# Three edits in a one-core decoder layer: list scatters without mutual waits, expert loads in pieces, an earlier start of cross attention

## The chip, the cores and the metric

The kernel runs on one core of a Trainium2 chip, as one program. A core has TensorE (PE in the profile; PEld is its weight load, which overlaps the matmuls), VectorE (DVE), ScalarE (ACT), GpSimd (POOL) and SyncE (SP, which here only issues DMAs). Each engine works through its own list of instructions in a fixed order. Engines meet through semaphores.

The metric is device time in microseconds (us), from launch to end. The inputs are float32, and the output must agree with the reference.

## The reference

One decoder layer on x of shape (4, 512, 512), which is 2048 tokens of width 512, in three residual parts:

```
x = x + deltanet(layernorm(x))            # gated delta rule, 16 heads of 128, causal convolutions
x = x + cross_attention(layernorm(x), ctx)    # 16 heads of 32, 256 context rows, fake-quantised q, k, v, weights
x = x + ffn(layernorm(x))
# ffn(t): 
h  = rmsnorm(t, ln1);  q, k, v = h @ wq, h @ wk, h @ wv     # 16 heads on 4 key/value heads of 128
x1 = t + causal_softmax(rope(rmsnorm(q)), rope(rmsnorm(k))) @ v @ wo
h2 = rmsnorm(x1, ln2)
sig = sigmoid(h2 @ router_w);  top 2 of 8 experts by sig + bias;  weights sig / sum
x1 + sum over the 2 experts of weight * (silu(h2 @ wg[e]) * (h2 @ wu[e])) @ wd[e]
```

Each token goes to two of eight experts. Which tokens an expert gets depends on the data.

## The kernel before

The tokens are 16 tiles of 128 (NT = 16), four to a sequence. The program has three stages in time.

**The first part** (0 to about 2190 us) is the delta rule, in pairs of heads, sequence by sequence. Cross attention of tiles 0 and 1 runs beside its end.

**The middle part** (about 2190 to 3650 us) is where all three edits act. Per tile i it has these generators, each of which issues a little work and yields:

- `cross(i)`: layernorm, the projection with wq, quantisation of q (`quantised`, whose last step is L217 on POOL), transposition through PE and ACT (`transposed`, L200 and L202), four rounds of scores, softmax over 256 context rows, quantisation of the weights (L274 on POOL, L278 on DVE), transposition (L287), product with the values (L300), projection (L318). `crossing(i)` also does `norms(i - 1)`, the two norms in front of the self attention of tile i - 1.
- `qkv(i)`: six projections of the tile (L1067) with weights that are loaded anew for each tile in halves of 512 KB into the four c_q buffers (L1034).
- `attention(i)`: scores (L1133), softmax, transposition (L1159), values (L1163), and the output projection (L1173) with weights loaded anew for each tile in eight pieces of 512 KB into three c_o buffers (L1043). Its last sum is L1199.
- `rest_of(i)`: the second norm, and the router's logits (L1230).
- `route(i0, n)`: the choice of experts for n tiles at a time, after tiles 3, 7, 11 (four tiles each), 14 (three) and 15 (one). DVE ranks the logits, PE counts places with small matmuls (L1257 to L1261), and then every token's two rows (its number and weight, 8 bytes) are scattered to their places in `lists` in HBM: one indirect DMA from POOL per tile and choice (L1282), so 8, 8, 8, 6 and 2 of them, 32 in all. `place` and `entry`, which hold rows and places, have two buffers each.
- `load_experts()`: waits until the last `crossing` and the last `qkv` have been issued, closes the pools `top` and `mid` that they used, and in the freed memory loads all weights of the eight experts: 24 DMAs of 512 KB on SP (L1305 to L1307).

**The last part** (from about 3640 us) gathers the lists (L1362 on POOL: one row of 128 entries for each of 39 blocks), gathers each block's tokens (L1388), applies the block's expert, and adds the result to `acc` in HBM. It ends with one copy to the output.

The order of the middle part is written out by `weave`. Every stream is a list of (start, length, generator, kind), in a virtual time whose unit is one tile of attention. A generator's steps are taken to be evenly spread over its length, with the step count of the last generator of its kind (`steps` has the first guess). `weave` always issues the step with the earliest virtual time. So attention(i) starts at i, qkv(i) at i - Q with Q = 1.36, crossing(i) at i - X with X = 2.75, rest_of(i) at i + 1.06, and load_experts at NT - Q = 14.64.

The order of issue is a priority, not yet the order on the engines. The framework lays out each engine's instructions ahead of time: among those whose inputs and buffers it takes to be ready, the one issued earliest comes first. So an instruction can stand much earlier on its engine than where it was issued. It also derives every wait from the tiles that are read and written. `lists` is one tensor for it, and so each scatter waits for the one before.

Of the kernel before, what the change touches and what calls it, by code (L numbers as in the profile page):

```python
# [40 lines left out]
NT = B * S // P  # L41
# [57 lines left out]
def decoder(ctx: ExitStack, tc: tile.TileContext, a: dict, out: bass.AP):  # L99
    nc = tc.nc  # L100
# [9 lines left out]
    def over(ap, n):  # L110

        return ap.unsqueeze(1).to_broadcast([P, n, ap.shape[1]])

    def along(ap, n):

        return ap.unsqueeze(2).to_broadcast([P, ap.shape[1], n])
# [22 lines left out]
    def chain(*gs):  # L139
        for g in gs:  # L140
            yield from g

    steps = {"cross": 38, "qkv": 12, "rest_of": 4, "route": 10, "load": 1}
    steps.update((f"attention{c}", n) for c, n in enumerate((37, 41, 53, 57)))

    def weave(*streams):


        todo = []
        for n, stream in enumerate(streams):  # L150
            stream = list(stream)
            todo.append([stream[0][0], n, 0, stream])
        while todo:
            t = min(todo, key=lambda t: t[:2])
            _, length, g, kind = t[3][0]
            try:
                next(g)
                t[0] += length / steps[kind]
                t[2] += 1
            except StopIteration:  # L160
                steps[kind] = max(t[2], 1)
                t[2] = 0
                del t[3][0]
                if t[3]:
                    t[0] = max(t[0], t[3][0][0])
                else:
                    todo.remove(t)
# [10 lines left out]
    def turns(*gs):  # L178

        gs = [(g, n) for g, n in gs if g is not None]  # L180
        while gs:
            left = []
            for g, n in gs:
                if all(next(g, gs) is not gs for _ in range(n)):
                    left.append((g, n))
            gs = left
            yield
# [774 lines left out]
    with ExitStack() as st:  # L962
# [37 lines left out]
        def norms(i):  # L1000


            x2 = x2s.pop(i)
            x3 = wq_.tile([P, D], F32, name="x3", bufs=1)
            yield from layernorm(x3.unsqueeze(1), x2.unsqueeze(1), small)
            nc.sync.dma_start(x3d[i], x3)
            h = wq_.tile([P, D], F32, name="h3", bufs=1)
            ss = small.tile([P, 1], F32, name="rms_s")
            nc.scalar.activation(h, x3, AF.Square, accum_out=ss)
            yield  # L1010
            r = small.tile([P, 1], F32, name="rms_r")
            rsqrt(r, ss, small, add=1e-6, mul=1.0 / D)
            yield
            nc.vector.scalar_tensor_tensor(h, x3, r, ln1, ALU.mult, ALU.mult)
            yield
            hTs[i] = transposed(h, wq_, "hT", bufs=2)
            yield
# [181 lines left out]
            nc.vector.tensor_tensor(x3, pw, x3, ALU.add)  # L1199
            xs[i] = x3  # L1200

        xs = {}
        lgt = keep.tile([P, NT, NE], F32, name="lgt")
        count = keep.tile([P, NE], F32, name="count")
        nc.vector.memset(count, 0.0)
# [28 lines left out]
        def route(i0, n):  # L1234

            shape = [P, n, NE]
            flat = lambda t: t.rearrange("p n e -> p (n e)")
            sig, key, w = (small.tile(shape, F32, name=k, bufs=1) for k in ("r_sig", "r_key", "r_w"))
            hot = [small.tile(shape, F32, name=f"r_hot{k}", bufs=1) for k in range(2)]
            m = small.tile([P, n], F32, name="r_m", bufs=1)  # L1240
            nc.scalar.activation(sig, lgt[:, i0 : i0 + n, :], AF.Sigmoid)
            nc.vector.tensor_tensor(key, sig, over(rb, n), ALU.add)

            for k in range(2):
                nc.vector.tensor_reduce(m, key, AX.X, ALU.max)
                nc.vector.tensor_tensor(hot[k], key, along(m, NE), ALU.is_equal)
                nc.vector.tensor_tensor(hot[k], hot[k], over(rank_row, n), ALU.mult)
                nc.vector.tensor_reduce(m, hot[k], AX.X, ALU.max)
                nc.vector.tensor_tensor(hot[k], hot[k], along(m, NE), ALU.is_equal)
                if k == 0:  # L1250
                    nc.vector.scalar_tensor_tensor(key, hot[0], MASKED, key, ALU.mult, ALU.add)
            nc.vector.tensor_tensor(key, hot[0], hot[1], ALU.add)
            yield

            pl = p_b.tile([P, n + 1, NE], F32, name="pb")
            for t in range(n):
                nc.tensor.matmul(pl[:, t, :], tab[:, C_BEFORE, :], key[:, t, :], start=True, stop=t == 0)  # L1257
                for u in range(t):
                    nc.tensor.matmul(pl[:, t, :], tab[:, C_ONES, :], key[:, u, :], start=False, stop=u == t - 1)
            for t in range(n):  # L1260
                nc.tensor.matmul(pl[:, n, :], tab[:, C_ONES, :], key[:, t, :], start=t == 0, stop=t == n - 1)  # L1261
            nc.vector.tensor_tensor(w, key, sig, ALU.mult)
            nc.vector.tensor_reduce(m, w, AX.X, ALU.add)
            nc.vector.reciprocal(m, m)
            nc.vector.tensor_tensor(w, w, along(m, NE), ALU.mult)
            base = small.tile([P, NE], F32, name="r_base", bufs=1)
            nc.vector.tensor_tensor(base, count, first_row, ALU.add)
            yield
            nc.vector.tensor_tensor(sig, pl[:, 0:n, :], over(base, n), ALU.add)
            nc.vector.tensor_tensor(count, count, pl[:, n, :], ALU.add)  # L1270
            place = small.tile([P, n, 2], mybir.dt.int32, name="r_place", bufs=2)
            entry = small.tile([P, n, 2, 2], F32, name="r_entry", bufs=2)
            for k in range(2):
                nc.vector.tensor_tensor(key, hot[k], sig, ALU.mult)
                nc.vector.tensor_reduce(m, key, AX.X, ALU.add)
                nc.vector.tensor_copy(place[:, :, k], m)
                nc.vector.tensor_copy(entry[:, :, k, 0], token[:, i0 : i0 + n])
                nc.vector.tensor_tensor(key, hot[k], w, ALU.mult)
                nc.vector.tensor_reduce(entry[:, :, k, 1], key, AX.X, ALU.add)
            for t in range(n):  # L1280
                for k in range(2):
                    nc.gpsimd.indirect_dma_start(  # L1282
                        lists[:, :],
                        bass.IndirectOffsetOnAxis(place[:, t, k : k + 1].bitcast(mybir.dt.uint32), 0),
                        entry[:, t, k, :],
                        None,
                        bounds_check=LISTS - 1,
                    )
                yield

        def crossing(i):

            g = cross(i)
            return chain(turns((norms(i - 1), 1), (itertools.islice(g, 6), 1)), g)

        def load_experts():

            while done[0] < 2:
                yield
            top.close()  # L1300
            mid.close()
            we = st.enter_context(tc.tile_pool(name="d_w", bufs=1, reuse_waits="tile"))
            gu, d = we.tile([P, NE, KD, 2, NI], F32, name="w_gu"), we.tile([P, NE, NI // P, D], F32, name="w_d")
            for e in range(NE):
                nc.sync.dma_start(gu[:, e, :, 0, :], a["d_wg"][e].rearrange("(k p) c -> p k c", p=P))  # L1305
                nc.sync.dma_start(gu[:, e, :, 1, :], a["d_wu"][e].rearrange("(k p) c -> p k c", p=P))
                nc.sync.dma_start(d[:, e, :, :], a["d_wd"][e].rearrange("(k p) c -> p k c", p=P))  # L1307
            experts_w.extend((gu, d))

        done, experts_w = [0], []  # L1310

# [3 lines left out]

        Q, X = 1.36, 2.75
        at_x = [(i - X, 1.0, crossing(i), "cross") for i in range(2, NT)]
        at_x[-1] = (*at_x[-1][:2], last(chain(at_x[-1][2], norms(NT - 1))), "cross")  # L1320
        at_q = [(i - Q, 1.0, qkv(i), "qkv") for i in range(NT)]
        at_q[-1] = (*at_q[-1][:2], last(at_q[-1][2]), "qkv")
        at_a = [(i, 1.0, attention(i), f"attention{i % TB}") for i in range(NT)]
        at_r = []
        for i in range(NT - 1):
# [4 lines left out]
                g, kind = chain(g, route(12, 3)), "route"  # L1330
            at_r.append((i + 1.06, 0.5, g, kind))
        run(norms(0))
        weave(at_a, at_q, at_x, at_r, [(NT - 1 - Q + 1, 0.1, load_experts(), "load")])
        w_gu, w_d = experts_w
        run(rest_of(NT - 1), route(NT - 1, 1))

# [22 lines left out]
        at = small.tile([P, 1], mybir.dt.int32, name="at", bufs=1)  # L1359
        nc.vector.tensor_copy(at, mine)  # L1360
        both_ = wa.tile([P, 4, P], F32, name="qT", bufs=6).rearrange("p a b -> p (a b)")[:, 0 : 2 * P]
        nc.gpsimd.indirect_dma_start(  # L1362
            both_[0:NBLK],
            None,
            lists.rearrange("(n s) c -> n (s c)", s=P),
            bass.IndirectOffsetOnAxis(at[0:NBLK, 0:1].bitcast(mybir.dt.uint32), 0),
            bounds_check=LISTS // P - 1,
        )
        nc.vector.tensor_scalar(be, be, float(NE - 1), None, ALU.min)
        who = small.tile([P, NBLK], mybir.dt.int32, name="who", bufs=1)  # L1370
        nc.vector.tensor_copy(who, be)
# [76 lines left out]
        for b in range(NBLK):  # L1448
            d = down(b)
# [65 lines left out]
```

## Time and profile before

| | |
|---|---|
| median of 3 runs | 3922.55 us (3909.57 to 3927.0) |
| the profiled execution | 3921.34 us, of which its span is 3919.6 us |
| mean granted clock of TensorE | 0.941 of full speed |
| POOL waited before L1282 for the landing of an earlier scatter | 62.8 us in 23 waits, the longest 5.1 us |
| landing of a scatter, from its issue | 2.2 to 7.8 us, median 5.2 us |
| landing of c_o loads, median | 4.1 us |
| landing of the expert loads, median by kind | 9.3, 10.0 and 9.6 us |

"Span" is from the first to the last instruction of the profiled execution. The profile page gives busy time by engine, the span in 40 slices, DMA queues, the chain that ended last, and groups of instructions with the idle time ahead of each and what ended it. In the notation `pb<-xnT,w` the tile left of the arrow is written, those right of it are read. A line `PE pb L200 <- POOL xn L217: 22.6, 5, 8.2` of the waits says that PE stood 22.6 us in total, 5 times, at most 8.2 us, ahead of instructions of line 200 that write `pb`, until POOL's line 217 had written `xn`. In a time line the columns are start, length, engine, line, operation, tiles, shapes and count, and in brackets the idle time ahead of it with what ended it.

The slices of the page, in fortieths of the span (98 us each), with PE's granted clock in tenths:

```profile
PE   5898899898989989898989799998998999897897
...
PEclk8899999899999998999999899998999999898898
```

The middle part begins at slice 23 of the 40.

### The profile page before, as it was taken

The page shows a single profiled execution, that of the slowest core. Times are in us where ns is not written, and L with a number is a line of the kernel's source. Part 1 is how long each engine was busy: PE and PEld are TensorE (multiplying, and loading weights), DVE is VectorE, ACT ScalarE, POOL GpSimd, SP SyncE. Part 2 cuts the span into 40 slices and gives each one's busy share as a digit, 9 for nine tenths or more (in the row PEclk, how much of TensorE's full clock was granted, in tenths as well). Part 3 has the DMA queues.
Part 4 walks back from the last instruction along what each step waited for, and adds up shares of the span by engine and source line. Part 5 has one row for each costly group of instructions (what it writes and reads, how often), then busy time and mean ns, then how long its engine had stood idle before and what let it go on. Part 6 is the DMA issues. An engine that isn't in the chain of part 4 may idle for free. (4 is left out here: it accounts for less than half of the span.)

```text
span 3919.6 us, 48951 instructions
## 1 busy us (share of the span) xinstructions
PE 3487.2 (89%) x16466; PEld 1984.1 (51%) x16466; DVE 2238.4 (57%) x5115; ACT 1522.5 (39%) x4190; POOL 1373.3 (35%) x1941
## 2 busy tenths in 40 slices
PE   5898899898989989898989799998998999897897
PEld 3455555555555555555555445554554555453343
DVE  5576657675766666756765466555665655543111
ACT  3434443334343434334333244443443444433121
POOL 1443554344435552455335222112212211210442
PEclk8899999899999998999999899998999999898898
DMA  5324332433243333343332444445444444445344
GB/s 163 107 77 123 98 103 80 130 101 111 82 119 119 98 100 106 97 119 104 96 98 87 158 145 154 137 132 132 146 127 137 153 146 139 141 152 183 79 82 93
DMA packets 391881, 465.56 MB, mean 119 GB/s; under 512 B 128451, under 2 KB 242115, under 8 KB 391440
## 3 DMA queue, kind: packets, MB, share of 16 engines
q1 hardware_dynamic: 380080, 438.03, 37.1%
q0 software_dynamic: 10112, 21.58, 3.1%
q8 instruction: 132, 2.16, 0.2%
q10 hardware_dynamic: 1440, 2.84, 0.2%
q14 instruction: 117, 0.96, 0.1%
HBM read 401.76 MB, written 64.81 MB: 119 GB/s over the span
## 5 line engine op out<-in xcount | busy, mean ns | idle before, releaser
L503 PE MATMUL pb<-xnT,w 128*128 128x512 f32 x2048 | 954.9, 605 | 0.0
L503 PEld LDWEIGHTS pb<-xnT,w 128*128 128x128 f32 x2048 | 381.9, 195 | 423.7 <-issue 419.7
L514 DVE SCALAR_TENSOR_TENSOR cv<-pb,pp,cv 128x511 f32<-128x511 f32 (+2 forms) x576 | 427.3, 742 | 153.0 <-ACT cv L511 144.2
L1067 PE MATMUL pb<-c_q,hT 128*128 128x512 f32 x768 | 362.9, 609 | 7.9 <-DMA c_q<-in_c_wq_dram 3.6
L644 POOL TENSOR_TENSOR iW<-iA,iT 32x31 f32<-32x31 f32 (+15 forms) x496 | 249.3, 503 | 210.3 <-DMA iA<-at_d 140.5
L825 PE MATMUL pb<-wot,og 128*128 128x512 f32 x512 | 264.9, 642 | 32.8 <-DVE og L796 26.5
L645 POOL TENSOR_TENSOR iT<-iT,iW 32x31 f32<-32x31 f32 (+15 forms) x496 | 275.1, 555 | 39.0
L1173 PE MATMUL pw<-c_o,oT 128*128 128x512 f32 x512 | 244.8, 611 | 21.9 <-DMA c_o<-in_c_wo_dram 15.5
L511 ACT ACTIVATE cv<-pb,pp 128x512 f32<-128x512 f32 x192 | 148.2, 772 | 261.2 <-PE pb L503 260.7
L1067 PEld LDWEIGHTS pb<-c_q,hT 128*128 128x128 f32 x768 | 143.8, 196 | 162.2 <-issue 149.4
L1139 ACT ACTIVATE e<-pb,nm,rq 128x128 f32<-128x128 f32 (+3 forms) x256 | 158.0, 626 | 104.2 <-DVE nm L1137 75.2
L274 POOL TENSOR_SCALAR x_e<-x_e 128x1024 f32<-128x1024 f32 x64 | 68.7, 1073 | 334.0 <-ACT x_e L269 256.6
L644 DVE TENSOR_TENSOR iW<-iA,iT 32x31 f32<-32x31 f32 (+15 forms) x496 | 178.4, 360 | 11.7 <-DMA iA<-at_d 0.2
L645 DVE TENSOR_TENSOR iT<-iT,iW 32x31 f32<-32x31 f32 (+15 forms) x496 | 177.4, 358 | 11.9
L269 ACT ACTIVATE x_e<-pb,nm 128x256 f32<-128x256 f32 x256 | 118.1, 475 | 164.2 <-DVE nm L266 160.7
L1163 PE MATMUL po<-eT,val 128*128 128x512 f32 x320 | 171.6, 630 | 10.0 <-ACT eT L1161 7.7
L1133 PE MATMUL pb<-kT,qT 128*128 128x256 f32 (+3 forms) x576 | 163.5, 410 | 3.6 <-ACT x_e L269 3.6
L558 POOL TENSOR_TENSOR rk<-ss,mhalf 128x8 f32<-128x8 f32 x32 | 53.1, 1659 | 322.0 <-DVE ss L557 321.9
L579 DVE SCALAR_TENSOR_TENSOR at<-pb,em 128x512 f32<-128x512 f32 x64 | 44.3, 692 | 199.9 <-ACT em L397 199.9
L1173 PEld LDWEIGHTS pw<-c_o,oT 128*128 128x128 f32 x512 | 94.4, 194 | 125.5 <-issue 92.1
L1420 PE MATMUL pb<-w_gu,eT 128*128 x312 | 142.7, 601 | 3.8 <-issue 3.8
L825 PEld LDWEIGHTS pb<-wot,og 128*128 128x128 f32 x512 | 89.7, 194 | 110.3 <-issue 53.3
(324 smaller groups left out, 6609.7 us busy)
## 6 DMA issues: line engine op xcount, KB each, us to landing
c_o<-in_c_wo_dram SPq DMA_DIRECT2D x128, 512.0 KB, 4.1
c_q<-in_c_wq_dram SPq DMA_DIRECT2D x128, 512.0 KB, 4.6
w<-in_a_w_dram SPq DMA_DIRECT2D x124, 512.0 KB, 3.7
row<-g_d SPq DMA_DIRECT2D x64, 512.0 KB, 3.8
at_d<-at SPq DMA_DIRECT2D x64, 256.0 KB, 4.2
T<-t_d SPq DMA_DIRECT2D x32, 512.0 KB, 6.1
X<-x_d SPq DMA_DIRECT2D x32, 512.0 KB, 6.1
rrow<-r_d SPq DMA_DIRECT2D x32, 512.0 KB, 4.7
```

The costliest lines, as they stand in the source:

```text
L503: nc.tensor.matmul(pj, wt[:, kd, p * P : (p + 1) * P], xnT[:, kd, :], start=kd == 0, stop=kd == KD - 1)
L511: nc.scalar.activation(ac, pj, AF.Identity, bias=cb[:, m, h : h + 1], scale=cw[:, m, h, 3:4])
L514: nc.vector.scalar_tensor_tensor(ac[:, j:], pj[:, : S - j], cw[:, m, h, 3 - j : 4 - j], ac[:, j:], ALU.mult, ALU.add)
L644: eng.tensor_tensor(u, A[:, i, i + 1 :].unsqueeze(2).to_broadcast([nb, n, w]), T[:, i, :w].unsqueeze(1).to_broadcast([nb, n, w]), ALU.mult)
L645: eng.tensor_tensor(T[:, i + 1 :, :w], T[:, i + 1 :, :w], u, ALU.add)
L825: nc.tensor.matmul(pw, og[p][:, c * P : (c + 1) * P], wot[:, p, :], start=p == 0, stop=p == HG - 1)
L1067: nc.tensor.matmul(pj, hT[:, kd, :], w[:, kd % 2, :], start=kd == 0, stop=kd == KD - 1)
L1133: nc.tensor.matmul(ps[:, m, k * P : (k + w) * P], qT[g][:, n + m, :], kT[:, g, j : j + w, :], start=True, stop=True)
L1139: nc.scalar.activation(e[n + m][:, :nk], ps[:, m, :nk], AF.Exp, bias=nm[:, n + m : n + m + 1], scale=rq, accum_out=es[:, n + m : n + m + 1])
L1163: nc.tensor.matmul(po, val[:, g, :], eT, start=k == 0, stop=k == c)
L1173: nc.tensor.matmul(pw, oT[:, h + m, :], w[:, m, :], start=g == 0 and h + m == 0, stop=g == 3 and h + m == 3)
L1420: nc.tensor.matmul(pg, hT[:, kd, :], w_gu[:, bass.ds(e, 1), kd, :, :], start=kd == 0, stop=kd == KD - 1)
```

## The change

There are three edits, and the diff is whole but for context.

1. The scatters of `route` are put into one group whose members need not wait for each other, with the reason that each row is written once. Their names are kept in `entered`. The gather of the lists gets an explicit dependence on each of the 32.
2. `load_experts` yields after every DMA, its tiles are handed out before the loads, and its stream gets the length 0.9 and 26 assumed steps where it had 0.1 and 1. Its start is the same number: NT - 1 - Q + 1 is NT - Q.
3. `crossing(i)` starts at 2 - 3.1 + (i - 2) 1.03 and has the length 1.03. It started at i - 2.75 with the length 1.

```diff
-    steps = {"cross": 38, "qkv": 12, "rest_of": 4, "route": 10, "load": 1}
+    steps = {"cross": 38, "qkv": 12, "rest_of": 4, "route": 10, "load": 26}
...
-        xs = {}
+        xs, entered = {}, []
...
-                    nc.gpsimd.indirect_dma_start(
+                    ins = nc.gpsimd.indirect_dma_start(
                         lists[:, :],
                         bass.IndirectOffsetOnAxis(place[:, t, k : k + 1].bitcast(mybir.dt.uint32), 0),
                         entry[:, t, k, :],
                         None,
                         bounds_check=LISTS - 1,
-                    )
+                    ).ins
+                    tc.declare_no_dep(ins, group="entries", reason="a row is written once")
+                    tc.add_to_no_dep_group("entries", ins)
+                    entered.append(ins.name)
                 yield
...
+            experts_w.extend((gu, d))
+
             for e in range(NE):
                 nc.sync.dma_start(gu[:, e, :, 0, :], a["d_wg"][e].rearrange("(k p) c -> p k c", p=P))
+                yield
                 nc.sync.dma_start(gu[:, e, :, 1, :], a["d_wu"][e].rearrange("(k p) c -> p k c", p=P))
+                yield
                 nc.sync.dma_start(d[:, e, :, :], a["d_wd"][e].rearrange("(k p) c -> p k c", p=P))
-            experts_w.extend((gu, d))
+                yield
...
-        Q, X = 1.36, 2.75
-        at_x = [(i - X, 1.0, crossing(i), "cross") for i in range(2, NT)]
+        Q, X, W = 1.36, 3.1, 1.03
+        at_x = [(2 - X + (i - 2) * W, W, crossing(i), "cross") for i in range(2, NT)]
...
-        weave(at_a, at_q, at_x, at_r, [(NT - 1 - Q + 1, 0.1, load_experts(), "load")])
+        weave(at_a, at_q, at_x, at_r, [(NT - Q, 0.9, load_experts(), "load")])
...
-        nc.gpsimd.indirect_dma_start(
+        ins = nc.gpsimd.indirect_dma_start(
             both_[0:NBLK],
             None,
             lists.rearrange("(n s) c -> n (s c)", s=P),
             bass.IndirectOffsetOnAxis(at[0:NBLK, 0:1].bitcast(mybir.dt.uint32), 0),
             bounds_check=LISTS // P - 1,
-        )
+        ).ins
+
+        for name in entered:
+            tc.add_manual_dep(ins, name, mybir.DependencyInfo(mybir.DependencyClass.Sync, mybir.DependencyReason.DATA), reason="entries")
```

## The prediction

> **What bounds the kernel now.** I read the busy rows first, then TensorE's waits in the last stage (2190 to 3650 us, where attention, projections, cross attention and routing are woven), then the time lines around each long wait.
>
> ```profile
> PE 3487.2 (89%) x16466; PEld 1984.1 (51%) x16466; DVE 2238.4 (57%) x5115; ACT 1522.5 (39%) x4190; POOL 1373.3 (35%) x1941
> ...
> PE pb L200 <- POOL xn L217: 22.6, 5, 8.2
> PE pw L1173 <- DMA c_o<-in_c_wo_dram: 15.5, 1, 15.5
> ...
> PE pb L287 <- DVE rsq L122: 9.1, 1, 9.1
> ```
>
> TensorE (PE) is busy 89%, and 93 to 100% in most 20 us windows of this stage, so the stage's time is PE's work plus its idle time. Two causes make most of that: c_o, and what comes over POOL. The POOL time line at the third full routing shows why:
>
> ```profile
> 3375.58 1.03 POOL L1282 DMA_INDIRECT lists<-r_entry,r_place  x1 [2.86 <-DMA lists<-r_entry,r_place]
> 3379.79 0.99 POOL L1282 DMA_INDIRECT lists<-r_entry,r_place  x1 [3.18 <-DMA lists<-r_entry,r_place]
> 3380.81 1.05 POOL L217 TENSOR_TENSOR xn<-xn,fq_s 128x512 f32<-128x512 f32 x1
> ```
>
> Each scatter waits for the landing of the one before, with POOL stopped; L217 stands behind five of them. PE then waits 8.2 us, and comes back at a lower clock:
>
> ```profile
> 3381.92 1.11 PE L200 MATMUL pb<-tab,xn 128*128 128x128 f32 x4 [8.25 <-POOL xn L217]
> ...
> 3360.00:3380.00 20.00, 13.67 (x42) 6.64 (x40) 8.82 (x30) 4.23 (x13) 6.51 (x8) 0.84 0.50 108
> 3380.00:3400.00 20.00, 18.08 (x56) 9.75 (x57) 8.19 (x18) 6.10 (x20) 7.29 (x9) 0.68 0.20 53
> 3400.00:3420.00 20.00, 19.89 (x78) 9.69 (x80) 9.95 (x23) 9.42 (x30) 4.98 (x6) 1.00 0.71 218
> ```
>
> (Window, length, busy PE, PEld, DVE, ACT, POOL, granted PE clock, DMA share, GB/s.) In the second row PE is busy 18.1 us, but at clock 0.68: four transposes take 1.11 us where 0.60 is usual.
>
> The other cause, on SP's queue and on PE:
>
> ```profile
> 3552.93 1.65 SPq L1307 DMA_DIRECT2D w_d<-in_d_wd_dram  x1
> 3554.68 13.11 SPq L1043 DMA_DIRECT2D c_o<-in_c_wo_dram  x4
> ...
> 3546.41 1.98 PE L1163 MATMUL po<-eT,val 128*128 128x512 f32 x4 [0.29 <-ACT eT L1161]
> 3563.90 3.49 PE L1173 MATMUL pw<-c_o,oT 128*128 128x512 f32 x4 [15.51 <-DMA c_o<-in_c_wo_dram]
> ```
>
> The 24 expert loads leave from 3523.71 to 3554.68; the c_o load that PE needs goes behind them and lands 9.2 us after (median 4.1).
>
> **The change, step by step** (against the profiled run, 3921.3 us).
>
> *Scatters.* Per routing I add PE's idle time, from its waits, and the excess of cold matmuls over the same rows at full clock.
> - First (2656 to 2724): waits 9.1+2.5+2.3+0.7+0.3 = 14.9; cold: L287 1.08 for 0.60, L1173 3.45 for 1.88 and 6.71 for 3.60, together 5.2. Sum 20.1.
> - Second (3012 to 3052): waits 8.1+1.8; cold L200, L1163, L262 2.0. Sum 11.9.
> - Third (3356 to 3404): wait 8.2; cold L200, L1159, L262, L1163, L1075 and eight L1067 (5.51 for 3.60), 5.8. Sum 14.0.
>
> Cold matmuls at 2655.87 and 3358.87 follow the routing's own small matmuls and stay.
>
> Afterwards a scatter costs POOL its issue only. The nearest row is that of the independent row gathers (L1388), 1.32 us apart (1.01 busy, 0.30 between). On generation the Trainium skill ("DMA: Bandwidth & Descriptors", Anatomy of one DMA) says many descriptors can be emitted before their cost shows; that would leave nothing of the stalls and give all 46.0. The row decides: eight scatters hold POOL 8 x 1.32 = 10.6 us, and POOL executes in order, so a part stays. In the second and third routing the block (3360.5 + 10.6 = 3371.1) ends before L217's input is due (about 3373): I leave 2 and 3. In the first, L274's input is ready near 2677 and the second half of the entries only at 2663.6 (VectorE), and DVE's copy into r_entry (L1277) still waits for the buffer's readers to land (9.07 us at 2703.06 now): I leave 5. Gain 15+10+11 = **36**; bounds -7 (three times a block of 10.6 for a stall of 8.2) and 46.
>
> On the cold part the skill ("TensorE: Matmul & The Clock Gate", Part 1) has a half clock after an idle window of about 3.4 us, for about one busy window. By that a gap over 3.4 us costs 1.7 us; three gaps 5.1, where the rows show 5.2+2.0+5.8 = 13.0. With the rule the routings would lose 38.1 instead of 46.0 in all and the gain be near 29. I take the rows: in the third, matmuls are still slow at 3389, seven us after the gap.
>
> *Expert loads in 24 steps.* The loads get virtual time 14.64 to about 15.5 instead of one instant. They wait for nothing but the freed pools, as before; a c_o load issued between them is ahead of later pieces. c_o's buffer was free at 3541.4 (L1173 from 3539.57, 1.88); 4.1 to 9.2 us later is 3545.5 to 3550.6, against PE's need at 3548.4. So of 15.5 + cold 1.6 (3.49 for 1.88) = 17.1 I leave 2: gain **15**, bounds 0 (c_o cannot go later than behind all 24, where it is now) and 17.1. Late next is route(12, 3), at 3579.84 (PE waits 2.27 for DVE), which moves with it. Traffic now is 313 and 360 GB/s in the two 20 us windows from 3520; the same 12.6 MB over some 60 us is 210, plus c_o. The pieces stand behind c_o loads that wait for PE (29.06 us for four from 3577.60), and the first expert matmul is at 3647.60: even the last piece, due at half of attention(15), about 3577, has 70 us.
>
> *End.* Two scatters and the gather are a chain: 3629.58, 3633.41, 3636.84. The second's entry is ready at 3631.0, so it goes 2.2 us sooner, and all that follows with it. The gather now waits for all 32 scatters by name. Behind it on POOL stand the 39 row gathers, and PE for those. Of the 32, 30 landed by about 3610; a satisfied wait costs about 0.05 us (median semaphore row of L1277), 1.6 us at most, inside the 2.44 us that the gather waits anyway. Gain **2**, bounds 0.6 and 2.2.
>
> *Cross attention.* Starts move from i - 2.75 to 1.03 i - 3.16: 0.35 tile sooner at i = 2, 0.04 later at i = 15. The last cross with its norms ends near 13.45, before qkv(15) at 13.64. Before attention 0 PE has gaps, and the longest is cross(2)'s own:
>
> ```profile
> 2260.37 1.12 PE L200 MATMUL pb<-tab,xn 128*128 128x128 f32 x4 [5.26 <-POOL xn L217]
> ```
>
> With 0.9+0.7+0.4 beside it, 7.2 us idle, and cold L200, L262, L1067 0.5+1.0+1.2 = 2.7: 9.9. Under qkv(0)'s matmuls (3.60 us a group) that chain is covered; but its loads (xi, 256 KB) and stores (x3d, x2d) enter SP's queue before c_q loads for which PE already waited 3.6 us at 2232. I take half, **5**, bounds -4 and 9.9.
>
> Sum 36+15+2+5 = **58**: 3921.3 - 58 = 3863; the median of the runs is 1.2 above the profiled run, so **3864**.
>
> **Rivals.**
> - *The loads still leave as a lump* (all 24 are ready at the same moment, and SP is idle between c_o loads, which speaks for it; that a c_o load goes ahead of later pieces speaks against). The 15 are lost: 3879.
> - *The scatters become a block that holds POOL*: 10.6 us is more than the 8.2 us stalls. For it: POOL's order is fixed beforehand, and eight scatters are ready together. Against: in two of three routings the block ends in time. 36 lost: 3900.
> - *Slower: cross attention falls badly against attention.* Each tile has one chain L217 to L200 like the prelude's, where PE stood 5.3 us; in steady tiles it is now under 1. If the new phase opens it in 14 tiles, 14 x 5.3 = 74, against a gain of 53 elsewhere: 3943. It decides from 53 / 14 = 3.8 us a tile on. Against it: the shift is at most 0.35 tile, and the chain keeps its length and its neighbours.
> - *All stalls go*: 46+17.1+2.2+9.9 = 75: 3847.
>
> **Chances.** Forecast 0.57, lump 0.17, block 0.14, all gone 0.06, slower 0.06. 0.5% (20 us) is about what a measurement can tell from no change; the block case lies at that edge, half of it within. Range 3843 to 3895: from all gone to near the block. Faster 0.87, same 0.07, slower 0.06.
>
> **What would show it.** L1282 about 1.3 us apart, no L1282 waiting for a landing; PE's waits on L217 near 22.6 - 16 - 5 = 2 us; clock rows of 1.00 where 0.68 to 0.84 stood; c_o loads between expert loads, and PE's 15.5 us wait under 3; the gather 5 us after the first scatter of the last routing instead of 7.3. Wrong if SP issues the 24 loads unbroken, if L217 or L274 stands behind six scatters or more, or if PE's waits in tiles without routing grow past 3.8 us.

## The result and the profile after

The changed kernel took **3872.77 us** (median of 6 runs, 3865.23 to 3880.07), the kernel before beside it 3922.27 us (6 runs): a ratio of 0.9877, 95% interval 0.9855 to 0.9899. The forecast was 3864.0, with a range of 3843 to 3895. In a later comparison the same changed kernel made 3864.12 against 3920.55 (0.9855, 0.984 to 0.987). So the change is worth some 50 to 56 us.

The profiled execution took 3875.28 us, its span 3873.5 us. Its busy row and its slices of TensorE (PE), with the granted clock:

```profile
PE 3479.9 (90%) x16466; PEld 1984.5 (51%) x16466; DVE 2238.7 (58%) x5115; ACT 1523.7 (39%) x4190; POOL 1374.0 (35%) x1941
...
PE   5898989898989898989889879999999999898897
...
PEclk8899999998999999999999889999999999999898
```

Slices 28 and 31 (first and second routing), which showed 8 before, show 9 now, and the 7 of slice 37 (c_o behind the expert loads) is an 8. Slice 35, the third routing, has kept its 8, and slice 24, in front of attention 0, has fallen from 9 to 7. PE's busy time is nearly the same (3487.2 before): what is gone is mostly idle time. PE's waits, longest sums first, from 2190 us to the end of the routing (engine, tile and line that waited, what it waited for, then total, times, longest):

```profile
PE pb L287 <- DVE x_e L278: 18.9, 5, 5.2
PE pb L200 <- POOL xn L217: 16.4, 3, 9.8
...
PE pb L262 <- ACT x_qT L202: 4.4, 3, 3.5
```

Two things are to be seen. The 15.5 us behind c_o are gone: no row for it is left. But the wait on L217, forecast near 2 us, is still 16.4, and its longest grew from 8.2 to 9.8. That longest wait is again at the third full routing; the other 6.6 us lie in front of attention 0 and just behind it (4.77 at 2256 us, 1.87 at 2320), as do four of the five waits of L287. At the second routing the 8.1 us of before are gone, and a wait of 3.5 on L202 (third row) stands there. The time line of all engines at the third:

```profile
3347.69 0.97 POOL L1282 DMA_INDIRECT lists<-r_entry,r_place  x1 [0.30 <-issue]
3348.67 0.47 POOL L995 TENSOR_TENSOR rope_s<-q,tab 128x128 f32<-128x128 f32 x1
3349.59 0.42 DVE L998 TENSOR_TENSOR q<-rope_c,rope_s 128x256 f32<-128x256 f32 x1 [5.68 <-POOL rope_s L996]
3355.98 0.21 DVE L1277 COPY r_entry<-tab 128x1 f32<-128x1 f32 x2 [5.10 <-DMA lists<-r_entry,r_place]
3359.99 0.42 DVE L216 TENSOR_SCALAR xn<-xn 128x512 f32<-128x512 f32 x1
3361.76 1.12 PE L200 MATMUL pb<-tab,xn 128*128 128x128 f32 x4 [9.77 <-POOL xn L217]
```

This is the main reading of the case. The scatters no longer wait for each other; they follow at 1.28 us, and POOL is done with seven of them at 3348.66. Yet POOL's L217 runs only at 3360.55, because its input, L216 on DVE, comes at 3359.99. DVE had stood twice: 5.68 us for the rotary product on POOL (L995, L996), which the fixed order put behind seven scatters, and 5.10 us for the landing of a scatter that still reads the buffer into which L1277 copies for the routing after the next (two buffers take turns; the single column is that of the last routing). PE's wait is entered under POOL, the last link; the two gaps that made it stand on DVE.

Windows of the changed kernel (window, length, busy PE, PEld, DVE, ACT, POOL, granted PE clock, DMA share, GB/s), two around that place and one in the middle of the expert loads:

```profile
3340.00:3360.00 20.00, 11.76 (x45) 6.34 (x43) 7.95 (x29) 6.55 (x16) 9.47 (x11) 0.91 0.46 106
3360.00:3380.00 20.00, 18.24 (x54) 9.67 (x55) 11.72 (x28) 7.83 (x29) 3.62 (x5) 0.75 0.26 76
...
3520.00:3540.00 20.00, 19.15 (x86) 11.25 (x84) 13.15 (x49) 10.86 (x22) 1.82 (x2) 1.00 1.05 354
```

The clock falls to 0.75 in the second row, as it did after the gap before the change. The clock record of these traces knows two values, 1.0 and 0.5, and here it stands at 0.5 from 3356.41 to 3370.06: it falls inside the gap, and 8.3 us of PE's work behind the gap run at half speed.

```profile
3356.41:3370.06 13.65, 8.30 (x22) 4.43 (x23) 7.60 (x20) 6.00 (x18) 1.85 (x2) 0.50 0.00 1
```

In the third row of the windows above PE is busy 19.15 us at full clock while 354 GB/s come in, expert weights for the most part. SP's queue shows why they harm nobody now:

```profile
3534.28 0.99 SPq L1043 DMA_DIRECT2D c_o<-in_c_wo_dram  x1
3535.31 0.66 SPq L1314 DMA_DIRECT2D w_d<-in_d_wd_dram  x1
```

c_o pieces (L1043) go out between expert pieces.

**Where the time went, tile by tile.** Attention ends with one sum per tile on DVE (L1199). I took its start for each tile, from the DVE time lines of two kernels, and subtracted; the difference at the first L320 (near 2160 us, the same program until there) is taken off. Minus is sooner than before. The three full routings lie between tiles 3 and 4, 7 and 8, 11 and 12, the expert loads between 13 and 14.

| us against before, at tile | 3 | 4 | 7 | 8 | 11 | 12 | 13 | 14 | 15 |
|---|---|---|---|---|---|---|---|---|---|
| changed kernel | +9.8 | -9.4 | -17.2 | -20.6 | -21.2 | -22.7 | -23.5 | -47.8 | -47.6 |
| scatters alone | -0.5 | -11.9 | -11.9 | -11.8 | -11.8 | -14.5 | -14.5 | -14.5 | -14.5 |
| loads alone | +0.1 | +0.5 | +2.1 | +5.2 | +5.1 | +3.1 | +3.1 | -21.1 | -19.7 |
| cross attention alone | +9.4 | +5.1 | -2.7 | -5.0 | -5.6 | -9.4 | -10.2 | -9.8 | -10.3 |
| scatters and loads | -1.0 | -14.4 | -14.5 | -14.0 | -14.1 | -15.9 | -15.9 | -40.2 | -40.0 |

The last four rows are experiments. With cross attention moved, tile 3's sum is not a measure of work done: PE has done more cross attention ahead of it. From tile 12 on the rows can be read as gains. Differences of some 5 us are not safe: PE, POOL, DVE and ACT have the same instructions in the same order before the change and with the loads alone up to 3541 us, and yet that row has drifted to +5.2 at tile 8.

**Idle time and half clock.** A second count splits what PE loses at the three full routings (the stretches from tile 3's sum to tile 4's, 7 to 8 and 11 to 12 together) into idle time and half clock, which is half of PE's busy time while the clock record stands at 0.5.

| us, three routings together | PE idle | lost to half clock |
|---|---|---|
| kernel before | 42.0 | 22.5 |
| scatters alone | 27.1 | 24.5 |
| scatters and loads | 29.0 | 21.5 |
| changed kernel | 21.5 | 16.6 |
| changed kernel, five buffers | 14.6 | 20.4 |
| changed kernel, scatters doubled | 42.0 | 20.4 |
| routing every two tiles | 5.9 | 0.0 |
| the same, with the other pace | 8.9 | 3.1 |

The count closes: from the first L320 to tile 15's sum, PE's busy time less this loss is 1289 us both before and after, so the 47.6 us of the table are, within 0.1, 41.9 of idle time and 5.8 of clock. It also shows that an idle gap taken away need not take the half clock with it.

### The profile page after: what moved, and what is told of

It is laid out like the page before. It is cut to its first block, busy times and chain, and to the rows that moved or that the text cites. A ratio compares the mean times of both kernels' runs of the same rounds, so it can differ in the third digit from the quotient of the medians.

```text
span 3873.5 us, 48929 instructions
## 1 busy us (share of the span) xinstructions
PE 3479.9 (90%) x16466; PEld 1984.5 (51%) x16466; DVE 2238.7 (58%) x5115; ACT 1523.7 (39%) x4190; POOL 1374.0 (35%) x1941
## 5 line engine op out<-in xcount | busy, mean ns | idle before, releaser
L1067 PE MATMUL pb<-c_q,hT 128*128 128x512 f32 x768 | 360.7, 608 | 7.4 <-DMA c_q<-in_c_wq_dram 3.4
L1067 PEld LDWEIGHTS pb<-c_q,hT 128*128 128x128 f32 x768 | 143.5, 195 | 165.4 <-issue 152.3
L274 POOL TENSOR_SCALAR x_e<-x_e 128x1024 f32<-128x1024 f32 x64 | 68.7, 1074 | 329.4 <-ACT x_e L269 240.4
L645 DVE TENSOR_TENSOR iT<-iT,iW 32x31 f32<-32x31 f32 (+15 forms) x496 | 176.0, 355 | 11.9
L1163 PE MATMUL po<-eT,val 128*128 128x512 f32 x320 | 170.2, 625 | 6.9 <-ACT eT L1161 3.8
L995 POOL TENSOR_TENSOR rope_s<-q,tab 128x128 f32<-128x128 f32 x64 | 35.4, 552 | 319.7 <-DVE q L1097 281.0
L397 ACT ACTIVATE em<-em,ee 128x128 f32<-128x128 f32 x256 | 78.6, 388 | 172.4 <-POOL ee L560 172.4
```

Source lines behind the costliest of these rows:

```text
L645: eng.tensor_tensor(T[:, i + 1 :, :w], T[:, i + 1 :, :w], u, ALU.add)
L1067: nc.tensor.matmul(pj, hT[:, kd, :], w[:, kd % 2, :], start=kd == 0, stop=kd == KD - 1)
L1163: nc.tensor.matmul(po, val[:, g, :], eT, start=k == 0, stop=k == c)
```

## The experiments

Each is compared with the kernel before, run beside it on the same chip.

**The three edits one by one.** Scatters alone:

```diff
-                    nc.gpsimd.indirect_dma_start(
+                    ins = nc.gpsimd.indirect_dma_start(
...
+                    tc.declare_no_dep(ins, group="entries", reason="a row is written once")
+                    tc.add_to_no_dep_group("entries", ins)
+                    entered.append(ins.name)
```

> The kernel before with the scatters' edit alone (no waits between the scatters, the gather waits for all). Theory A, the prediction's sum: the routings give 36 us and the end 2, so 38 in all, about 3884. Theory B, from the trace of after: the scatters no longer wait, but in two of three routings PE still stands (9.8 us and 3.5 + 1.4 us), because eight scatters hold POOL together and because VectorE's copy into r_entry waits for their landing; then this edit alone gives 15 to 25 us, 3897 to 3907, and PE's waits behind L217 and L278 at the routings stay over 8 us in at least one of them.

Measured: 3895.72 against 3917.16 us, 0.9948 (0.9931 to 0.9966), 13 to 27 us by the interval, 14.5 by the table. The routings gained 11.4, -0.1 and 2.7 us in the table, where 15, 10 and 11 were forecast. The size is theory B's; that a wait would stay over 8 us did not come (the longest is 7.20). The second routing, which gained nothing, on POOL, DVE and PE:

```profile
3008.92 0.98 POOL L1282 DMA_INDIRECT lists<-r_entry,r_place  x1 [0.30 <-issue]
3009.91 0.47 POOL L995 TENSOR_TENSOR rope_s<-q,tab 128x128 f32<-128x128 f32 x1
3010.83 0.42 DVE L998 TENSOR_TENSOR q<-rope_c,rope_s 128x256 f32<-128x256 f32 x1 [5.45 <-POOL rope_s L996]
3013.92 0.24 DVE L1277 COPY r_entry<-tab 128x3 f32<-128x3 f32 x2 [2.54 <-issue]
3018.82 1.05 POOL L217 TENSOR_TENSOR xn<-xn,fq_s 128x512 f32<-128x512 f32 x1 [6.33 <-DVE xn L216]
3019.92 1.11 PE L200 MATMUL pb<-tab,xn 128*128 128x128 f32 x4 [7.20 <-POOL xn L217]
```

and the same place before the change:

```profile
3018.63 0.47 POOL L995 TENSOR_TENSOR rope_s<-q,tab 128x128 f32<-128x128 f32 x1
3019.54 0.43 DVE L998 TENSOR_TENSOR q<-rope_c,rope_s 128x256 f32<-128x256 f32 x1 [1.05 <-POOL rope_s L996]
3024.41 0.43 DVE L216 TENSOR_SCALAR xn<-xn 128x512 f32<-128x512 f32 x1
3032.84 1.05 POOL L217 TENSOR_TENSOR xn<-xn,fq_s 128x512 f32<-128x512 f32 x1
```

Before, L995 stood behind two scatters and L217 behind five: L217 ran 8.0 us after L216 had ended (3024.84). Now L995 stands behind all eight, and DVE waits 5.45 + 2.54 us where it waited 1.05: 6.9 more. Counted from the first scatter of the routing (3012.57 and 2999.45), PE's L200 comes after 21.4 us before and after 20.5 us now. The stall moved from POOL to DVE. (For the 2.54 us the profile names no releaser, but the semaphore row of L1277 there takes 2.77 us, and the scatters' landings end at 3013.65, just ahead of it.) PE is idle 2.7 us less between the sums of tiles 7 and 8, and the half clock took that back: 8.5 us are lost to it there, before 5.4.

Loads alone:

```diff
-        weave(at_a, at_q, at_x, at_r, [(NT - 1 - Q + 1, 0.1, load_experts(), "load")])
+        weave(at_a, at_q, at_x, at_r, [(NT - Q, 0.9, load_experts(), "load")])
```

with the yields and the step count of the change.

> The kernel before with the expert loads' edit alone. Theory A: 15 us (15.5 wait and 1.6 cold, less 2), about 3907. Theory B: the wait of 15.5 us takes 1.6 us of cold matmuls and about 6 more of small waits and cold matmuls at the routing behind it with it, so 23 to 25 us, about 3898; SP's c_o loads stand between the expert loads.

Measured: 3892.37 against 3917.16, 0.9936 (0.9916 to 0.9957), 17 to 33 us; 24.2 us between tiles 13 and 14 in the table. The larger value was right; the terms are in the next section.

Cross attention alone:

```diff
-        Q, X = 1.36, 2.75
-        at_x = [(i - X, 1.0, crossing(i), "cross") for i in range(2, NT)]
+        Q, X, W = 1.36, 3.1, 1.03
+        at_x = [(2 - X + (i - 2) * W, W, crossing(i), "cross") for i in range(2, NT)]
```

> The kernel before with the earlier and longer cross attention alone. Theory A: 5 us faster, about 3917. Theory B: the chain L217 to L200 of tile 2 is not covered (4.8 us in after, 5.3 before), so the earlier start gives nothing in front of attention 0: 3918 to 3926, no change.

Measured: 3909.18 against 3917.16, 0.9982 (0.9972 to 0.9992), 3 to 11 us; 10.3 in the table. The size fits the forecast 5, but not the place: in front of attention 0 the transposes L200 and L287 still wait 4.47, 3.11 and 4.17 us, where before one wait of 5.26 stood, and PE is busy 46.67 us at clock 0.83 from 2240 to 2300 us, before 51.77 at 0.94.

By their medians the three single edits make 21.4 + 24.8 + 8.0 = 54 us, all three together 50 and 56 in the two comparisons. They nearly add.

**Without the third edit** (the first two together), beside the changed kernel itself once more: this asks what the third is worth where it was applied.

```diff
-        Q, X, W = 1.36, 3.1, 1.03
-        at_x = [(2 - X + (i - 2) * W, W, crossing(i), "cross") for i in range(2, NT)]
+        Q, X = 1.36, 2.75
+        at_x = [(i - X, 1.0, crossing(i), "cross") for i in range(2, NT)]
```

> The kernel after without the edit of the cross attention's start (scatters and loads only). Theory A (the earlier start covers a chain in front of attention 0, wherever the scatters are): about 5 to 8 us slower than after. Theory B (alone it gained by moving the cross chains off the waiting scatters of the routings; with those waits gone nothing is left to gain): as after within 3 us; PE idle in front of attention 0 is not larger than in after.

> The kernel after itself, on the same chip as the runs beside it, as their base: 0.9877 of before within its interval, 3865 to 3880.

Measured side by side: without it 3876.48 (0.9885, 0.987 to 0.9901), the changed kernel 3864.12. The third edit is worth 12 us there, more than either theory had, and 7.6 in the table. Two windows of the changed kernel in that run, the stretch in front of attention 0 and a stretch between routings:

```profile
2240.00:2300.00 60.00, 47.45 (x215) 25.84 (x213) 28.04 (x57) 20.27 (x60) 13.53 (x19) 0.80 0.34 112
...
2400.00:2640.00 240.00, 237.80 (x1056) 127.08 (x1053) 139.46 (x351) 109.89 (x302) 46.45 (x66) 1.00 0.46 146
```

and without the edit:

```profile
2240.00:2300.00 60.00, 52.11 (x265) 29.18 (x263) 34.91 (x83) 26.66 (x83) 14.48 (x21) 0.91 0.46 157
...
2400.00:2640.00 240.00, 229.21 (x1019) 121.55 (x1018) 135.56 (x341) 109.76 (x302) 43.05 (x62) 0.99 0.44 141
```

Busy time times clock is PE's work at full speed. In front the edit loses 52.11 x 0.91 - 47.45 x 0.80 = 9.5 us; in the 240 us between it gains 237.80 - 229.21 x 0.99 = 10.9, and from 2720 to 2980 another 7.2 (256.33 at 1.00, without it 251.63 at 0.99). And the second count has the three routings better too, 29.0 of idle time falling to 21.5 and 21.5 of half clock to 16.6. So the gain lies in the steady tiles and at the routings, and in front there is a loss.

**The loads as a lump again.** All else as in the changed kernel, its yields too; only the stream's length in virtual time differs:

```diff
-        weave(at_a, at_q, at_x, at_r, [(NT - Q, 0.9, load_experts(), "load")])
+        weave(at_a, at_q, at_x, at_r, [(NT - Q, 0.01, load_experts(), "load")])
```

> The kernel after, with 0.01 in place of 0.9 as the length of the expert loads' stream: the pieces are still issued one by one, but all before any later c_o load. Theory A (it is the place of the c_o loads among the pieces that counts): the 24 leave unbroken, PE's c_o wait of some 15 us is back and with it all of the loads' gain, so 23 to 25 us slower than after, about 3897. Theory B (breaking the issue up is enough, since SP would have let ready c_o loads pass): as after.

Measured: 3890.72, 0.9934 (0.992 to 0.9947), 27 us slower than the changed kernel beside it; by the table's count it loses 24.8 us against it between tiles 13 and 14. PE waits 15.7 us for c_o, and SP's queue has it behind all 24 pieces, the last of which leaves at 3522.07:

```profile
3533.04 3.78 PE L1173 MATMUL pw<-c_o,oT 128*128 128x512 f32 x4 [15.70 <-DMA c_o<-in_c_wo_dram]
3523.82 13.40 SPq L1043 DMA_DIRECT2D c_o<-in_c_wo_dram  x4
```

So it is the place of c_o among the pieces that counts, not that there are yields.

**Each scatter twice**, the second copy into a list that nobody reads:

```diff
+    spare = dram.tile([LISTS, 2], F32, name="spare")
...
+                    ins = nc.gpsimd.indirect_dma_start(
+                        spare[:, :],
...
+                    tc.declare_no_dep(ins, group="spare", reason="a row is written once")
```

> The kernel after with every scatter followed by a second one of the same rows into a spare list that nobody reads: 32 more scatters on POOL, nothing waits for their result but the buffers. Theory A (the block's time on POOL is covered in two of three routings): 5 us slower or less. Theory B (POOL's block of 8 x 1.3 us is what is left of the stalls): each full routing holds POOL 10 us longer and PE stands 5 to 10 us longer in each, so 15 to 30 us slower than after.

Measured: 3897.75, 0.9941 (0.9928 to 0.9955), 34 us slower than the changed kernel beside it, where theory B had 15 to 30. Between tiles 3 and 4, 7 and 8, 11 and 12 it loses 12.5, 6.0 and 6.3 us against the changed kernel. 32 more scatters of 1.28 us are 41 us of POOL. But the run does not show that PE pays for POOL's block as such: the second copies read the same buffers, so the landing on which L1277 waits (L1278 in this kernel) is doubled up too. At the third routing the rotary product stands behind seven scatters again, at the same distance from the first (9.2 us), and DVE waits 5.66 us for it as in the changed kernel; what grew is the wait of the copy:

```profile
3379.08 0.22 DVE L1278 COPY r_entry<-tab 128x1 f32<-128x1 f32 x2 [9.53 <-DMA spare<-r_entry,r_place]
3382.24 1.11 PE L200 MATMUL pb<-tab,xn 128*128 128x128 f32 x4 [15.71 <-POOL xn L217]
```

At the second it is 10.68 us, against 6.02. At the first, DVE's two waits for L274 on POOL make 8.4 us, against 5.7, and the copy's 5.03, against 4.54.

**Five buffers for places and entries**, so that L1277 waits for no landing:

```diff
-            place = small.tile([P, n, 2], mybir.dt.int32, name="r_place", bufs=2)
-            entry = small.tile([P, n, 2, 2], F32, name="r_entry", bufs=2)
+            place = small.tile([P, n, 2], mybir.dt.int32, name="r_place", bufs=5)
+            entry = small.tile([P, n, 2, 2], F32, name="r_entry", bufs=5)
```

> The kernel after, with five buffers for r_place and r_entry in place of two, so that VectorE's copy of a later routing's tokens (L1277) never waits for the landing of scatters. Theory A (that copy costs nothing that counts): as after, 3873 within 3. Theory B: VectorE waited 4.5, 6.0 and 5.1 us there, and part of it reached PE: 5 to 12 us faster than after, 3861 to 3868, and PE's 9.8 us wait at the third routing falls by about 5.

Measured: 3864.53, 0.9872 (0.985 to 0.9894), no different from the changed kernel on the medians. Its table row ends at -51.6, that is 4 us sooner, which is within what two profiles of one order differ by. Yet PE's wait at the third routing fell from 9.77 to 3.09 us, so the copy's wait was the larger part of it. Why so little of this shows in the time, the stretch from tile 11's sum to tile 12's tells, first in the changed kernel, then here:

```profile
3310.80:3395.10 84.30, 72.21 (x344) 41.90 (x340) 47.53 (x136) 34.10 (x101) 23.04 (x28) 0.92 0.48 138
3296.70:3379.80 83.10, 77.70 (x344) 44.11 (x337) 47.08 (x133) 33.93 (x101) 23.05 (x28) 0.88 0.46 139
```

PE is idle 5.4 us in place of 12.1, but the granted clock is 0.88 in place of 0.92: 20 us at half clock, not 14, and more of PE's work in it. The half clock took back 5.6 of the 6.7 us. Why it did is not shown.

**The start and the pace of cross attention.** First the early start with the old pace, then the old start with half of the new pace:

```diff
-        Q, X, W = 1.36, 3.1, 1.03
+        Q, X, W = 1.36, 3.1, 1.0
```

> The kernel after with the cross attention's start 0.35 sooner but the old pace (length 1.0 for 1.03), so that it stays ahead to the end. Theory A (the earlier start is what gains): as after within 3 us. Theory B (the slower pace is what gains in the steady tiles, where PE's waits fell from 10.2 to 1.6 us between 2400 and 2640, while the start costs about 5 us of PE's idle time and its clock in front of attention 0): 8 to 12 us slower than after, no faster than the kernel without the edit of the cross attention.

```diff
-        Q, X, W = 1.36, 3.1, 1.03
+        Q, X, W = 1.36, 2.75, 1.015
```

> The kernel after with the old start of cross attention (2.75 ahead) and a slightly slower pace (1.015 for 1.0; with more the last cross attention would end after its projections begin). Theory A (the earlier start gains): as without the edit of the cross attention, 8 to 12 us slower than after. Theory B (the pace gains): as after or up to 5 us faster, since the idle time in front of attention 0 stays near that of the kernel without the edit.

Measured: 3874.92 (0.986, 0.9845 to 0.9875), by the ratio as the changed kernel, but by the table's count 5.5 us behind it and 2 ahead of the kernel without the edit, so this run does not decide between its theories; and 3854.18 (0.9811, 0.9798 to 0.9825), 74 us faster than before and some 17 to 26 faster than the changed kernel by the ratios (20.6 by the table's count), more than either theory had. With the old start the front is whole again (51.95 us busy at 0.94 from 2240 to 2300), while the steady tiles keep their gain (236.68 us busy of the 240). A later start was better than the earlier one. Which part of the steady gain the pace makes and which the phase at the routings was not taken apart further; start 2.75 with pace 1.03 was not tried.

**Routing every two tiles**, as soon as they are there, the last two tiles singly, with a buffer for each of the nine calls:

```diff
-            if i in (3, 7, 11):
-                g, kind = chain(g, route(i - 3, 4)), "route"
+            if i % 2 and i < NT - 2:
+                g, kind = chain(g, route(i - 1, 2)), "route"
...
-                g, kind = chain(g, route(12, 3)), "route"
+                g, kind = chain(g, route(NT - 2, 1)), "route"
```

> The kernel after with routing after every two tiles in place of four (four scatters at a time, nine buffers for r_place and r_entry; the last two tiles one by one). Theory A (what is left at the routings is no matter of the block's length): 3 us slower to 3 faster, more small VectorE work against nothing. Theory B (the block of eight and VectorE's copy behind it cost 15 to 20 us of PE's time over three routings): the block is 5.2 us and mostly covered, so 5 to 12 us faster than after in spite of four more routings of some 30 small VectorE instructions each.

Measured: 3839.93 against 3927.91, 0.9779 (0.9766 to 0.9793): 88 us faster than before, some 30 to 38 faster than the changed kernel (by the ratios; 37 by the table's count). Its windows at the three former routings, then its line L1277 over the whole middle part:

```profile
2640.00:2720.00 80.00, 78.58 (x375) 44.94 (x374) 56.41 (x163) 41.59 (x118) 22.92 (x30) 1.00 0.59 178
...
2980.00:3040.00 60.00, 58.27 (x288) 33.09 (x287) 40.93 (x103) 30.50 (x92) 17.50 (x23) 1.00 0.59 175
...
3320.00:3400.00 80.00, 77.26 (x353) 43.21 (x352) 45.26 (x109) 36.13 (x108) 17.32 (x24) 1.00 0.56 165
```

```profile
L1277 DVE COPY r_entry<-tab x18: 117/162/666, 2201.3 to 2204.8; 128x2 f32<-128x2 f32 x14, 128x1 f32<-128x1 f32 x4
```

No window stands below 1.00 any more: PE is busy 58.27 of 60 us where the changed kernel in the other control run has 55.85 at clock 0.86. With a buffer each, all 18 copies of L1277 run at 2201 to 2205 us, ahead of everything, and wait for nobody. Four scatters in a row hold POOL 5 us instead of 10, and DVE has no wait over 1 us for the rotary product any more. By the second count the three routings lose 15.6 us less to idle time and 16.6 less to half clock than in the changed kernel: about half of the gain is the clock, which both theories had left out. The buffers alone gave 4 us in the table (the run above), so the gain needs the smaller batch, or batch and buffers together; pairs with two buffers were not tried.

**Both together**, as the version to keep:

```diff
-        Q, X, W = 1.36, 3.1, 1.03
+        Q, X, W = 1.36, 2.75, 1.015
```

on top of the routing in pairs.

> The changed kernel with both variants that were faster than it: routing for every two tiles as soon as they are there (nine buffers for places and entries, the last two tiles singly), and cross attention at 2 - 2.75 + (i - 2) 1.015 with length 1.015. Alone they made 87 us (ratio 0.978) and 74 us (0.981) against the kernel before, and the changed kernel makes 57 us (0.9855) in the same kind of comparison, so they are worth some 30 and 17 us beyond it. Theory A: they act at different places (routing in pairs: the waits and the cold clock at the three routings; the pace: the stretch in front of attention 0 and the tiles between routings), so their gains add: about 0.973 of the kernel before (0.971 to 0.975), near 3818 us where the kernel before takes 3925, with TensorE idle in the middle part below 80 us. Theory B: the pace gained mostly at the second and third routing, where its windows also improved (56.0 us busy from 2980 to 3040 and 74.0 from 3320 to 3400, against 55.9 and 69.2 before), and pairs have already cured these: within 5 us of the pairs alone, 0.977 to 0.979, 3833 to 3845 us.

Measured: **3824.47** against 3917.59 us, 0.9767 (0.9746 to 0.9788): 93 us faster than before, the fastest version of all. The gains do not add: the ratio is at the edge of theory B's, 0.977, and only the end of its interval reaches theory A's 0.975 (the time itself lies between the two named, 3818 and 3833 to 3845, with the kernel before at 3917.59 here). TensorE is idle 69.4 us from 2184 to 3555, the middle part of this kernel, so theory A's sign, under 80, did come. By the table's count it is 15 us ahead of the pairs alone at tile 3 (part of it cross attention not yet done), but 4 us at tile 15: at the routings the pace gains nothing more on top of the pairs, and by the second count it costs 6 us there. The gain, 9 us by the same count, lies ahead of tile 3's sum.

## Why the prediction was right in sum and wrong in its terms

58 us were forecast, 50 to 56 came. The sum was right because wrong terms cancel: too much for the scatters, too little for the loads and cross attention. That is luck, not the mechanism.

- **Scatters: 36 forecast, about 15 to 21 measured.** The step that failed is that at the second and third routing the block "ends before L217's input is due (about 3373): I leave 2 and 3". The block (8 x 1.28 us) was sized rightly and does end in time. But the forecast took the due time of L217's input from the kernel before, as if it were fixed. That input comes from DVE, and DVE waits for POOL too: the rotary product L995 now stands behind seven scatters or all eight, where single scatters used to leave it gaps. At the third routing L216 ended 12.7 us after the first scatter before, and 20.9 us after it now. So the sign "L1282 about 1.3 us apart" came true, and the one of waits on L217 near 2 us did not (16.4); the sign of being wrong that was named, L217 behind six scatters or more, came true, with all eight ahead of it, though the block itself was long over. The other cost, the wait of L1277 for landings, was named, but only in the first routing; it rose from 11.0 to 15.7 us in all three. At the first routing, with no such chain in the way, 11.4 of the forecast 15 came. The cold matmuls are a second mis-sized term: the forecast let 13.0 us of them go with the waits, but with the scatters alone 24.5 us are lost to half clock at the three routings, before 22.5, so only idle time was gained (42.0 to 27.1).
- **Loads: 15 forecast, 24 measured.** The mechanism is as forecast, c_o between the pieces. The term was mis-sized because only c_o's wait and the cold matmuls right behind it were counted. In the trace before, from the sum of tile 13 to that of tile 15, PE was idle 20.9 us, after it 1.9: with the 15.5 went 3.5 us of small waits behind it (route(12, 3) had 2.27, now 0.63, where "which moves with it" was forecast). The rest of the 24 is clock, 4.9 us of half clock before and none after: at that routing the ten transposes L1159 took 2.38 us, now 1.29, and four L1163 3.03, now 1.98. The forecast that spreading lowers the traffic to 210 GB/s was wrong: 333 and 354 GB/s in two windows, at no cost to PE.
- **End: 2 forecast, 0.45 measured.** From the first scatter of the last routing to the gather were 7.26 us, now 6.81. The second scatter leaves 2.1 us sooner, but from its start to the gather it is 5.09 us, before 3.43: its landing takes 3.85 us, before 2.53, and the gather's longer row of semaphores adds 0.3.
- **Cross attention: 5 forecast, 8 to 12 measured**, by another mechanism. The forecast let the earlier start fill PE's gap in front of attention 0; there it lost some 9 us. The gain comes later, in the steady tiles, which the forecast had treated only as a danger, and at the routings.

Of the rivals, the lump was rejected by the trace, and its price was shown to be 25 to 27 us, not 15. The POOL block turned out half true: with what hangs on it, DVE's wait for the rotary product and for the landings, it keeps about half of the 36 us. The slower case did not come: in the steady tiles PE waits less, not more (237.80 us busy of 240, without the edit 229.21). On the clock the Trainium skill ("TensorE: Matmul & The Clock Gate", Part 1) gives about one busy window of 3.4 us at half clock after an idle window. For the length of the slow spell the rows were the better guide: after the 9.77 us gap at 3361.76 eight L1067, running to 3372, still take 4.91 us for 3.60, and the record stands at half clock for 8.3 us of busy PE. For the gain neither was: the rule would have made it near 29 (28 with the remainders of 5, 2 and 3), the rows 36, and 15 to 21 came, with less idle time gone than either supposed and the half clock still there. Likewise the skill's "DMA: Bandwidth & Descriptors" (Anatomy of one DMA) says that many descriptors can be emitted before their cost shows; here each scatter of 128 rows holds POOL 1.28 us, and seven in a row make DVE wait 5.68 us for the rotary product behind them.

## What to carry to other kernels

When a wait is taken away, do not take the due times of what stands behind it from the old trace: ask what each of its inputs in turn waits for on the engine that is now kept busy without a break. Small batches of work that holds one engine, with a buffer of their own each, were worth more here (30 to 38 us) than removing the waits inside a large batch (15 to 21). For the loads that share a queue with an urgent one, the place in the queue counted here, not the traffic. When an idle gap is closed and the time does not follow, compare the granted clock over the stretch. When a generator is moved, look at the steady tiles as well as at the gap that it should fill.

## What was not expected of the hardware

- The first part of the kernel, the same program in each of these kernels, ended between 9.8 us sooner and 2.6 us later than in the profiled run of before (at the first L320). So single profiles tell a few us apart only if differences are taken inside the middle part. Even there, profiles with the same order of instructions agree within 0.5 us at every tile in one case (the changed kernel in its two comparisons) and differ by 5.2 in another (before and loads alone, at tile 8).
- A scatter's landing took 2.2 to 7.8 us before (median 5.2), and 3.1 to 10.0 us (median 6.0) when eight leave in a row, but with the scatters alone the median was 3.9 (2.8 to 10.1). The longest grew in both; the median moved either way and was used for nothing.
